# Two products trade places in the first group, and two heads trade buffers: a LoRA layer and paged attention on one core

## The chip, the core and the metric

The kernel runs on one core of a Trainium2 chip. A core has five engines that run side by side: TensorE (PE) for matrix products, VectorE (DVE), ScalarE (ACT), GpSimd (POOL) and SyncE (SP), which here only issues DMAs. ACT and POOL issue DMAs too. The metric is device time in microseconds for one execution, and the median over several runs is what counts.

## The reference

Two layers stand behind each other, each with a residual. For 8 sequences of 128 tokens with 512 features:

```python
x = x + einsum('bsi,boi->bso', x, weight[adapter_ids])      # one 512x512 adapter per sequence
# second layer, on the new x
q, k, v = x @ Wq.T, x @ Wk.T, x @ Wv.T                       # 32 query heads, 8 KV heads of 128
q, k = rope(rmsnorm(q, q_norm_w), pos), rope(rmsnorm(k, k_norm_w), pos)
k_all, v_all = concat(k_cache[block_table], k), concat(v_cache[block_table], v)   # 512 + 128 keys
probs = softmax(where(valid, q @ k_all.T * SCALE, -1e30))    # a cached key counts if below seqlen
x = x + (probs @ v_all).reshape(...) @ Wo.T
```

Everything is float32. Four query heads share one KV head.

## The kernel before

**Groups and steps.** The 8 KV heads are cut into 4 groups of 2, with 8 query heads each. A step is one group for one sequence, so there are 32 steps; step `i` has group `g = i // 8` and sequence `b = i % 8`. All sequences of a group come before the next group. Group 0 also does the first layer: its step `b` computes the first layer of sequence `b + 2` (`lora_y`, PE writes `y`, four matmuls in the source, eight on the chip, since a float32 product takes two passes).

**A step** has 8 heads, `h` = 0 to 7. Each head's scores (`sc`, L1037) go to PE; DVE adds the mask and takes the minimum (L1047), ACT takes the exponential (L1063), POOL divides by the sum (L1110), and DVE turns 32x32 blocks (`turn_p`, L886, to `tp`). Four heads of one KV head make a unit. When its fourth head is turned, SP sends four DMAs (`exchange`, L806) that finish the transposition from `tp` to `pT`. `pT` is 128 by 2560 floats, 1.3 MB.

**What PE does between the scores** is a list, `main`, whose pieces are dealt out over the 8 heads by a cost that is written into the code. For steps 1 to 5 its order is: the values of the first KV head of the step before (`values(i-1, 0)`: ten matmuls `o`, which read `pT`), the projections of the next step's keys and values and its first queries, `lora_y(b + 2)`, the values of the second KV head (`values(i-1, 1)`), the next step's second queries, and the output projection of the step before. In steps 6 and later (`early`) both values stand later. PE works through its list in this order; so does every other engine with its own.

**Buffers of turned probabilities.** The pool `pts` holds one `pT`. Up to step 4 both KV heads use it: the first head's `pT` of step `i`, which SP issues in head 5, must wait until `values(i-1, 1)` has read the last one; the second head's, issued in head 1 of the next step, waits for `values(i, 0)`. From step 5 on (`u.i >= B - 3`) there is a second buffer, the tile `raw` of the pool `lora`. It holds the adapter's rows until their last transposes (`turn_lora`, PE `lw`) in step 5. `move` picks the buffer.

**SP's order** in a step: in head 0 the second keys (`move_k(i, 1)`, `kT`), in head 1 the second queries (`qT`) and the last unit's `pT`, in head 4 the next step's first keys, in head 5 the first unit's `pT`, in head 6 the next step's first queries and new keys (`send_q`: DVE turns them to `tq`, L828, then four DMAs `qT<-tq`), and in group 0 x of a later sequence (`load_x(b + 3)`). SP waits in this order: a DMA behind a waiting one isn't issued. The new keys come with `qT`; ACT copies them into place (`copy_k`, L778) in head 7, and the next step's scores need that copy.

**Other transfers.** POOL gathers pages of the caches (`kc`, `vc`) and the adapter's rows (`gather_lora`, head 6); ACT loads, turns and stores weights for the next group.

Of the kernel before, what the change touches and what calls it, by code (L numbers as in the profile page):

```python
# [19 lines left out]
B = 8  # L20
# [32 lines left out]
def lora_then_paged_attention(  # L53
# [22 lines left out]
    def pool(name, bufs=1, **kw):  # L76
        return ctx.enter_context(tc.tile_pool(name=name, bufs=bufs, **kw))
# [5 lines left out]
    lora = pool("lora")  # L83
# [6 lines left out]
    pts = pool("pts")  # L90
# [45 lines left out]
    raw = {}  # L136


    first = {}
# [416 lines left out]
    def group(name, pieces, after, width=HID):  # L556

        y = [None]

        def piece(k, operands):  # L560
            if k == 0:
                if len(pending) > 1:
                    run(pending)
                y[0] = ps_mm.tile([P, HID], FP, tag="mm", name=name)[:, 0:width]
            lhsT, rhs = operands()
            nc.tensor.matmul(y[0], lhsT=lhsT, rhs=rhs, start=(k == 0), stop=(k == len(pieces) - 1))  # L566
            if k == len(pieces) - 1:
                after(y[0])

        return [(UNIT, lambda k=k, o=o: piece(k, o)) for k, o in enumerate(pieces)]  # L570
# [16 lines left out]
    def lora_y(b):  # L587
        def after(y):
            def add():
                a = acc[b].rearrange("s (p j) -> s j p", j=4)  # L590
                nc.vector.tensor_tensor(a, y.rearrange("s (j p) -> s j p", j=4), a, ALU.add)

            pending.append(add)

        return group(
            f"y_{b}",
            [
                lambda c=c: (x1T[b][:, c, :], wT["lora"][:, c, :, :].rearrange("k j p -> k (j p)"))
                for c in range(KC)
            ],  # L600
            after,
        )
# [107 lines left out]
    def project(i, what):  # L710
        g, b = steps[i]
        s = st[i]

        def after_kv(y):

            s.q[0] = work.tile([P, 4 + GK, D], FP, tag="q0", name=f"q_{i}_0")
            s.k = s.q[0][:, 4 : 4 + GK, :]
            s.vn = news.tile([P, GW], FP, tag="vn", name=f"vn_{i}")
            s.ss = [
                small.tile([P, 6], FP, tag=f"ss{n}", name=f"ss_{i}_{n}") for n in range(2)  # L720
            ]

            def rest():
                nc.scalar.copy(s.vn, y[:, GW : 2 * GW])
                rotate(i, y, s.k, s.ss[0][:, 4:6], 1, 0)

            pending.append(rest)

        def after_q(n):
            def after(y):  # L730
                if n:
                    s.q[n] = work.tile([P, 4, D], FP, tag=f"q{n}", name=f"q_{i}_{n}")

                def rest():
                    rotate(
                        i,
                        y,
                        s.q[n][:, 0:4, :],
                        s.ss[n][:, 0:4],
                        0,  # L740
                        n,
                        lambda: norm_scales(i, n, 6 if n == 0 else 4),
                    )

                pending.append(rest)

            return after

        after = after_kv if what == "kv" else after_q(int(what[1]))
        return group(  # L750
            f"pj_{i}_{what}",
            [lambda c=c: (x1T[b][:, c, :], weights_of(what, c)) for c in range(KC)],
            after,
        )
# [48 lines left out]
    def exchange(dst, src):  # L803

        for b in range(4):
            nc.sync.dma_start(  # L806
                out=dst[:, b, :].unsqueeze(1), in_=src[Q4 * b : Q4 * b + Q4, :, :]
            )
# [15 lines left out]
    def send_q(i, n):  # L824
        s = st[i]
        heads = 4 if n else 4 + GK
        tq = work.tile([P, 4, heads, Q4], FP, tag=f"tq{n}", name=f"tq_{i}_{n}")
        nc.vector.transpose(tq, s.q[n].rearrange("p h (a d) -> p a h d", a=4))  # L828

        def move():  # L830
            s.qT[n] = qT_tile(i, n)
            exchange(
                s.qT[n].rearrange("d b h q -> d b (h q)"), tq.rearrange("p a h q -> p a (h q)")
            )

        to_read.append((now[0], 0, move))
# [3 lines left out]
    def values(i, j, at_once=False):  # L840

        s = st[i]

        def operands(c):
            pT = s.pT[j].rearrange("p b r (c q) -> p c (b r) q", c=NC)
            v = s.vc[:, c, :] if c < LC else s.vn
            return v[:, j * D : (j + 1) * D], pT[:, c, :, :]

        def after(o):
            s.oT[j] = work.tile([P, REP, S], FP, tag=f"oT{j}", name=f"oT_{i}_{j}")  # L850

            def copy():
                nc.scalar.copy(s.oT[j].rearrange("p h s -> p (h s)"), o)  # L853

            if at_once:
                copy()
            else:
                pending.append(copy)

        return group(f"o_{i}_{j}", [lambda c=c: operands(c) for c in range(NC)], after)  # L860

    def output(i, half=None):
        g, b = steps[i]
        s = st[i]
        cols = slice(0, 16) if half is None else slice(8 * half, 8 * half + 8)
        return group(
            f"out_{i}",
            [
                lambda h=h: (s.oT[h // 4][:, h % 4, :], weights_of(f"o{h // 4}", h % 4)[:, cols, :])
                for h in range(GQ)  # L870
            ],
            add_to_acc(b, g == G - 1, half),
            HID if half is None else HID // 2,
        )
# [26 lines left out]

    def move(u):

        pl, tag = (lora, "raw") if u.j and u.i >= B - 3 else (pts, "pT")
        pT = pl.tile([P, 4, REP, QK], FP, tag=tag, name=f"pT_{u.i}_{u.j}")
        exchange(pT.rearrange("p b r k -> p b (r k)"), u.tp.rearrange("p a r k -> p a (r k)"))
        st[u.i].pT[u.j] = pT
# [79 lines left out]
    for i, (g, b) in enumerate(steps):  # L987
        s = st[i]
        main = []
# [17 lines left out]
            main += values(i - 1, 0)  # L1007
        if i == last:
            main += output(i - 2)
        if g == 0 and b + 2 < B and i:  # L1010
            main += lora_y(b + 2)
        if i and not early:
            main += values(i - 1, 1)
        if i < last:
            main += project(i + 1, "q1")
        if early and i < last:
# [9 lines left out]
        for h in range(8):  # L1026
# [39 lines left out]
            if prev is not None:  # L1066
                u, pr = prev
                if u.i < last or u.j == 0:
                    turn_p(u, pr)
                if pr == REP - 1:  # L1070
                    to_read.append((8 * i + h, 1, lambda u=u: move(u)))
# [116 lines left out]
```

## Time and profile before

| | us |
|---|---|
| median of three runs (1225.03 to 1226.6) | 1226.48 |
| the profiled execution | 1226.99 |
| its span, first to last instruction | 1225.2 |
| PE busy | 1183.1 |
| DVE, ACT, POOL busy | 745.4, 534.4, 674.0 |
| PE busy with scores (L1037) | 324.7 |
| steps 2 to 5, length of each | 49.5, 48.9, 47.4, 47.3 |
| a step of group 1 (400.00 to 437.70) | 37.7 |

PE's mean granted clock is 0.987 of full speed. A row of a timeline gives the start, the length, the engine, the line of the kernel and the operation with its output and inputs; "SPq" is SP issuing a DMA, whose length is the time to issue, not to land. In brackets stands how long the engine was idle before and what ended the wait. A row of windows gives the stretch, its length, each engine's busy time and instructions, the granted clock, the DMA engines' busy share and what they moved. Names such as `pT` cover every tile of that name. The records of DMA packets in the trace have a queue, a start, a length and a size, and the sizes tell the transfers apart (`pT` 2560 bytes, `qT` with keys 768, `kT` 512, x 2048, the adapter's rows 8192).

### The profile page before, as it was taken

The page shows a single profiled execution, that of the slowest core. Times are in us where ns is not written, and L with a number is a line of the kernel's source. Part 1 is how long each engine was busy: PE and PEld are TensorE (multiplying, and loading weights), DVE is VectorE, ACT ScalarE, POOL GpSimd, SP SyncE. Part 2 cuts the span into 40 slices and gives each one's busy share as a digit, 9 for nine tenths or more (in the row PEclk, how much of TensorE's full clock was granted, in tenths as well). Part 3 has the DMA queues.
Part 4 walks back from the last instruction along what each step waited for, and adds up shares of the span by engine and source line. Part 5 has one row for each costly group of instructions (what it writes and reads, how often), then busy time and mean ns, then how long its engine had stood idle before and what let it go on. Part 6 is the DMA issues. An engine that isn't in the chain of part 4 may idle for free.

```text
span 1225.2 us, 13384 instructions
## 1 busy us (share of the span) xinstructions
PE 1183.1 (97%) x3354; PEld 577.5 (47%) x3354; DVE 745.4 (61%) x1675; ACT 534.4 (44%) x1648; POOL 674.0 (55%) x780
## 2 busy tenths in 40 slices
PE   7898979889899999999999999999999999999998
PEld 5553544444444444444444444444444444444445
DVE  5565646355556776666666776766666656656651
ACT  4563433434344444444444444444444444444442
POOL 5465445254465666555565666555566666555541
PEclk9999989889999999999999999999999999999999
DMA  7376466565597797767797787766797776655642
GB/s 283 104 192 172 122 177 169 156 169 134 142 236 178 205 250 192 176 173 201 171 241 183 203 254 187 177 182 189 174 238 181 184 201 148 150 138 149 150 116 60
DMA packets 173952, 217.59 MB, mean 178 GB/s; under 512 B 19508, under 2 KB 112436, under 8 KB 172980
## 3 DMA queue, kind: packets, MB, share of 16 engines
q1 hardware_dynamic: 111072, 128.76, 45.5%
q10 hardware_dynamic: 49524, 48.12, 12.4%
q0 software_dynamic: 13280, 39.86, 10.1%
q8 instruction: 28, 0.46, 0.2%
q14 instruction: 48, 0.39, 0.1%
HBM read 80.74 MB, written 17.83 MB: 80 GB/s over the span
## 4 chain that ended last, share of the span: by engine, by line
PE 92%; DMA 4%; ACT 1%; SPq 1%; DVE 1%; issue 1%; POOL 0%; ACTq 0%; DVEq 0%; POOLq 0%
PE sc L1037 23%; PE o L566 23%; PE pj_q L566 18%; PE out L566 15%; PE pj_kv L566 9%; DMA qT<-tq 3%; PE y L566 2%; PE lw L481 1%; DMA kT<-tk 1%; PE x L481 1%; SPq L806 1%; DVE p L1047 0%; PE wt_q L499 0%; PE wt_kv L499 0%; PE qt L793 0%
## 5 line engine op out<-in xcount | busy, mean ns | idle before, releaser
L1047 DVE CUSTOM_DVE_ANT_0 p<-sc,mask 128x640 f32<-128x640 f32 x256 | 210.9, 824 | 383.9 <-PE sc L1037 383.5
L1063 ACT ACTIVATE p<-p,mn 128x640 f32<-128x640 f32 x256 | 211.9, 828 | 331.6 <-DVE mn L1047 321.2
L1037 PE MATMUL sc<-kT,qT 128*128 128x512 f32 (+1 forms) x1024 | 324.7, 440 | 26.8 <-ACT kT L778 25.8
L1110 POOL TENSOR_SCALAR p<-p,rc 128x640 f32<-128x640 f32 x252 | 201.6, 800 | 268.6 <-DVE rc L1103 264.4
L1037 PEld LDWEIGHTS sc<-kT,qT 128*128 128x128 f32 x1024 | 194.2, 193 | 262.2 <-issue 226.9
L566 PE MATMUL o<-pT,vc 128*128 128x512 f32 x512 | 239.1, 597 | 0.0
L566 PE MATMUL pj_q<-w_q,x1T 128*128 128x512 f32 x512 | 236.8, 593 | 0.7 <-ACT w_q L500 0.7
L566 PE MATMUL out<-w_o,oT 128*128 128x512 f32 (+1 forms) x528 | 235.0, 580 | 0.9 <-ACT oT L853 0.7
L886 DVE STREAM_TRANSPOSE tp<-p 128x640 f32<-128x640 f32 x252 | 210.8, 836 | 4.1 <-POOL p L1110 3.9
L685 POOL TENSOR_TENSOR q<-q,sw 128x512 f32<-128x512 f32 (+1 forms) x89 | 96.8, 1087 | 98.8 <-DVE sw L668 98.6
L617 POOL DMA_INDIRECT kc<-in_L_cond_k_cache_dram,key_ix x128 | 130.7, 1021 | 32.8 <-issue 32.5
L617 POOL DMA_INDIRECT vc<-in_L_cond_v_cache_dram,val_ix x128 | 127.3, 995 | 31.1 <-issue 29.9
L566 PEld LDWEIGHTS out<-w_o,oT 128*128 128x128 f32 x528 | 95.7, 190 | 93.5 <-issue 85.4
L566 PEld LDWEIGHTS pj_q<-w_q,x1T 128*128 128x128 f32 x512 | 92.4, 190 | 92.7 <-issue 90.1
L566 PEld LDWEIGHTS o<-pT,vc 128*128 128x128 f32 x512 | 93.1, 193 | 89.8 <-issue 87.9
L698 ACT ACTIVATE q<-q,rs 128x128 f32<-128x128 f32 x256 | 81.8, 390 | 106.0 <-POOL q L685 93.9
L566 PE MATMUL pj_kv<-w_kv,x1T 128*128 128x512 f32 x256 | 116.6, 593 | 0.7 <-ACT x1T L483 0.7
L651 ACT ACTIVATE sq<-pj_q 128x128 f32<-128x128 f32 x256 | 70.7, 276 | 64.7 <-PE pj_q L566 39.7
L693 POOL TENSOR_TENSOR rs<-ss,mhalf 128x6 f32<-128x6 f32 x64 | 77.0, 1203 | 5.3
L566 PEld LDWEIGHTS pj_kv<-w_kv,x1T 128*128 128x128 f32 x256 | 46.0, 190 | 45.6 <-issue 44.7
L566 PE MATMUL o<-pT,vn 128*128 128x512 f32 x128 | 65.4, 593 | 0.0
L1103 DVE RECIPROCAL rc<-sm 128x1 f32<-128x1 f32 x256 | 33.4, 130 | 46.0 <-ACT p L1063 46.0
(123 smaller groups left out, 834.3 us busy)
## 6 DMA issues: line engine op xcount, KB each, us to landing
pT<-tp SPq DMA_DIRECT2D x252, 320.0 KB
kT<-tk SPq DMA_DIRECT2D x248, 64.0 KB
qT<-tq SPq DMA_DIRECT2D x116, 96.0 KB
qT<-tq SPq DMA_DIRECT2D x120, 64.0 KB
st_q<-in_L_cond_Wq_dram ACTq DMA_DIRECT2D x24, 256.0 KB
xw_q<-tw_q ACTq DMA_DIRECT2D x24, 256.0 KB
st_o<-in_L_cond_Wo_dram ACTq DMA_DIRECT2D x24, 256.0 KB
xw_o<-tw_o ACTq DMA_DIRECT2D x24, 256.0 KB
```

Of the source, the lines that this page charges most:

```text
L566: nc.tensor.matmul(y[0], lhsT=lhsT, rhs=rhs, start=(k == 0), stop=(k == len(pieces) - 1))
L617: nc.gpsimd.indirect_dma_start(out=dst[:, c, :], out_offset=None, in_=src, in_offset=bass.IndirectOffsetOnAxis(ap=rows[:, g, at : at + 1], ...
L651: nc.scalar.activation(sq, t[:, h, :], AF.Square, scale=float(D) ** -0.5, accum_out=ss[:, h : h + 1])
L685: add.tensor_tensor(dst, cw, sw[:, 0:heads, :], ALU.add)
L693: nc.gpsimd.tensor_tensor(rs[:, 0:width], ss[:, 0:width], mhalf[:, 0:width], ALU.pow)
L698: nc.scalar.activation(q, q, AF.Identity, scale=rs[:, h : h + 1])
L886: nc.vector.transpose(u.tp[:, :, r, :], u.p.pop(r).rearrange("q (a k) -> q a k", a=4))
L1037: nc.tensor.matmul(sc[:, lo:hi], lhsT=s.qT[j][:, r, 0:4, :].rearrange("d h q -> d (h q)"), rhs=s.kT[j].rearrange("d a c i -> d (a c i)")[: ...
L1047: nc.vector.tensor_tensor_reduce(out=p, in0=sc[:, 0:LA], in1=mask.rearrange("p a c i -> p (a c i)"), scale=1.0, scalar=3.0e38, op0=ALU.add ...
L1063: nc.scalar.activation(p, p, AF.Exp, bias=unit.mn[:, one], scale=-1.0, accum_out=unit.sm[:, one])
L1103: nc.vector.reciprocal(unit.rc[:, one], unit.sm[:, one])
L1110: nc.gpsimd.tensor_scalar(q, p, unit.rc[:, one], 1.0, ALU.mult, ALU.mult)
```

## The change

In steps 1 to 4 `values(i-1, 1)` comes ahead of `lora_y(b + 2)`. In step 5 (`b + 3 == B`) the order stays. From step 5 on the buffer `raw` takes the first KV head's `pT` and the buffer of `pts` the second's, where it was the other way round. Steps 0 and 6 to 31 keep their order.

```diff
     def move(u):
 
-        pl, tag = (lora, "raw") if u.j and u.i >= B - 3 else (pts, "pT")
+        pl, tag = (lora, "raw") if u.j == 0 and u.i >= B - 3 else (pts, "pT")
         pT = pl.tile([P, 4, REP, QK], FP, tag=tag, name=f"pT_{u.i}_{u.j}")
...
         if i == last:
             main += output(i - 2)
-        if g == 0 and b + 2 < B and i:
-            main += lora_y(b + 2)
+        first = lora_y(b + 2) if g == 0 and b + 2 < B and i else []
+        if b + 3 == B:
+            main += first
         if i and not early:
             main += values(i - 1, 1)
+        if b + 3 < B:
+            main += first
         if i < last:
             main += project(i + 1, "q1")
```

## The prediction

> **What bounds the kernel now.** I read the page first: PE is busy 1183.1 of 1225.2 us, so only its 42.1 us of idling can be won, plus what a lowered clock costs. Then PE's waits: one line holds 25.8 us of the 42.1.
>
> ```profile
> PE sc L1037 <- ACT kT L778: 25.8, 5, 6.6
> ```
>
> Five times PE waits for ACT's copy of the new keys (`copy_k`, L778). PE's timeline puts them ahead of the first scores of steps 2 to 6: 5.19, 6.38, 6.57, 3.94 and 3.68 us. Here is step 2 (from 121.48 us) up to the second of them; columns are start, length, engine, line, operation.
>
> ```profile
> 141.67 1.88 PE L566 MATMUL y<-wT,x1T 128*128 128x512 f32 x4
> 144.91 1.88 PE L566 MATMUL y<-wT,x1T 128*128 128x512 f32 x4
> 146.62 2.74 PE L566 MATMUL o<-pT,vc 128*128 128x512 f32 x6
> 149.20 1.24 PE L1037 MATMUL sc<-kT,qT 128*128 128x512 f32 x4
> 150.28 1.02 PE L566 MATMUL o<-pT,vc 128*128 128x512 f32 x2
> 151.14 1.02 PE L566 MATMUL o<-pT,vn 128*128 128x512 f32 x2
> 161.03 3.60 PE L566 MATMUL out<-w_o,oT 128*128 128x512 f32 x8
> 171.00 2.50 PE L1037 MATMUL sc<-kT,qT 128*128 128x512 f32 x4 [6.38 <-ACT kT L778]
> ```
>
> The first layer's product `y` runs, then the second KV head's values `o`, done at 152.16; PE runs dry at 164.63. SP's issues in the same stretch:
>
> ```profile
> 131.96 5.50 SPq L806 DMA_DIRECT2D pT<-tp  x4
> 140.18 2.48 SPq L806 DMA_DIRECT2D kT<-tk  x4
> 152.19 5.00 SPq L806 DMA_DIRECT2D pT<-tp  x4
> 157.30 5.73 SPq L806 DMA_DIRECT2D qT<-tq  x4
> 163.07 0.61 SPq L104 DMA_DIRECT2D acc<-in_x_dram  x1
> 163.78 5.86 SPq L806 DMA_DIRECT2D kT<-tk  x4
> ```
>
> The turned probabilities of step 2's first heads (`pT`, 152.19) go out 0.03 us after `o` has ended, though their source `tp` was ready at 148.21 (DVE, L886, 147.38 and 0.83 long): the one buffer of `pts` still held the last step's second heads. The next step's queries (`qT`) stand behind `pT` in SP's order; their packets end at 169.72, and ACT's copy, which needs the keys in them, starts at 170.54. (ACT's row names `kT<-tk` there; but in all five cases the copy follows `qT`'s last packet by 0.6 to 0.8 us.) Last, the steps and their sums (length, busy PE, PEld, DVE, ACT, POOL, granted clock, DMA share, GB/s):
>
> ```profile
> 121.48:171.00 49.52, 43.15 (x124) 21.68 (x125) 25.93 (x53) 18.52 (x56) 21.43 (x24) 0.91 0.62 168
> 171.00:219.86 48.86, 42.30 (x124) 21.11 (x125) 26.66 (x54) 18.47 (x56) 21.61 (x24) 0.95 0.59 158
> 219.86:267.26 47.40, 43.45 (x125) 21.79 (x125) 24.85 (x53) 18.47 (x56) 21.44 (x24) 0.93 0.59 158
> 267.26:314.58 47.32, 43.64 (x125) 21.90 (x125) 24.73 (x52) 18.57 (x56) 20.67 (x23) 0.93 0.57 143
> 314.58:353.40 38.82, 38.15 (x101) 18.44 (x102) 22.08 (x52) 17.74 (x56) 22.54 (x26) 0.96 0.68 183
> 400.00:437.70 37.70, 37.70 (x103) 17.84 (x102) 26.85 (x61) 16.73 (x54) 21.58 (x25) 1.00 0.81 210
> ```
>
> After each wait PE runs at half clock for a while (2 us windows show 0.50): four scores take 2.29 us to the next operation instead of 1.08. A step of this kind needs 40.7 us of PE at full clock; what the first four rows hold above that is the clock: 2.45 + 1.6 + 2.75 + 2.95 us, and some 1.5 us in the fifth. So the boundaries cost 25.8 + 0.7 (a wait of 0.67 us for x1T behind the last) + 11.2 = **37.7 us**.
>
> **The change part by part.**
>
> *Values ahead of `y` in steps 1 to 4.* No instruction is added or dropped: ten `o` matmuls and eight `y` matmuls (0.43 us apart, `y` 3.44 us in all) trade places; neither issues a DMA, and PE's total is unchanged: zero. `o` now begins where `y` did and all of it fits ahead of the sixth head's scores (1.08 us), so it ends 4.5 us earlier: 99.3, 147.6, 196.3 and 246.3 us on the clock of the traced run, instead of 103.8, 152.2, 200.8 and 250.9.
>
> *What that releases.* `pT` then waits for `tp` instead (ready at 99.0, 148.2, 196.9, 246.9). So SP issues it at 99.3, 148.2, 196.9, 246.9: 4.5, 4.0, 4.0, 4.0 us sooner. Its 5 us of issuing end at about 104.3 to 251.9, just when `tq`, the source of `qT`, is ready (104.64, 153.79, 201.75, 251.98), so `qT` is issued 4.2, 3.5, 4.0 and 4.2 us sooner.
>
> *The buffers trade places from step 5.* No work is added. In step 5 the first heads' `pT` no longer waits for the values at 298.43; it needs the last transposes of the adapter's rows (`lw`, 289.66 and 0.60 long) and `tp` (294.49): 4.0 us sooner, `qT` 4.5 us sooner. From step 6 each head has one buffer as before: zero.
>
> *What that does at PE.* From `pT`'s issue to the scores took 17.6, 18.8, 19.0, 16.4 and 16.1 us; PE runs dry 17.0, 16.4, 16.4, 16.4, 16.4 us after the new issues. Worst end: `qT` keeps its time from issue to landing; then waits of 1.0, 2.9, 2.6, 0 and 0 us remain, 6.5 us. Best end: none. I take none, because the sources of the delay thin out: between 144 and 146 us the DMA engines move nothing and in 148 to 154 a third of their time, while in 154 to 170 they are 0.9 busy with `pT`, `qT`, the gathers for steps ahead and x at once. `pT` took 9.7 us of packets there, and 7.7 us where it was alone (133.16 to 140.83). The gathers are POOL's and keep their places relative to PE, so `pT` and `qT` go ahead of them.
>
> *What is late next.* (1) Just behind `qT` on SP comes x of the step after, used 1.5 us into the new step. Before, it ended 0.7 to 3.3 us after `qT`. The adapter's gather (1 MB; 164.34 to 169.68 us, POOL) is first turned some 4.5 us into the step. With the boundary closed these come 0 to 1.2 us late in four steps. They share one wait; I take 0.5 each, the middle: 2 us. (2) `o` now starts 10.7, 9.7, 9.7 and 9.7 us after its own `pT` was issued (131.96 against 141.67). That `pT`'s packets ended 9.8, 8.9, 8.8 and 8.4 us after issue, and a reader starts 0.6 to 0.8 us later: it just fits. In steps 6 and 7 the same transfer took 10.0 and 9.6 us (322.65 to 332.64, 341.06 to 350.67), so 0 to 1 us late: 0.5 each, 2 us. While PE waits there, `y`, the next projections and scores queue behind it, but all that they feed moves with them.
> (3) `y`'s addition on DVE (1.1 us, L591) moves out of the fifth head into the seventh, where DVE idles 1.7 to 3.4 us: zero; uncovered, 1.1 us a step. The copy of `o` on ACT (0.59 us) moves ahead by a head into 2.9 us of idle time: zero. The first layer's result is read only in the next step.
>
> *Does a short wait cost the clock?* The waits of 3.68 to 6.57 us all did; none shorter is in these steps, so the residual may cost from nothing up to 1.5 to 3 us each. In 2 us windows the clock falls 2.7 to 5.3 us after PE stops, so for half a microsecond I take nothing. The Trainium skill (TensorE: Matmul & The Clock Gate, Why this matters for your kernels) says the rate halves after idle gaps above about 3 us; the trace agrees with its 3.68 us. By that rule the worst end above stays free of it too.
>
> **Sum.** 37.7 - 2 - 2 = 33.7 us off the profiled execution's 1226.99 us (its span is 1225.2): 1193.3. The median of the three runs, 1226.48, is 0.5 lower: **1193 us**. Nothing below 1226.5 - 37.7 = 1188.8 can come of this.
>
> **Rivals.**
> *Fixed delays.* The queries' time from issue to landing stays and 6.5 us of boundary waits remain, with the 2 us at the values, and the two longer ones (2.9, 2.6) may still lower the clock for 1.6 to 2.95 us each: 37.7 - 8.5 - (0 to 5) = 24 to 29, so 1197 to 1202. For it: `qT`'s issue alone took 4.5 to 6.1 us behind `pT` against 2.48 when free. Against: the idle DMA time at 144 to 154.
> *DMA becomes the bound.* Shorter steps push about 8.3 MB (168 GB/s by 49.5 us) through 41 us: 203 GB/s. The values' `pT` then takes 11.4 us, the longest seen (299.67 to 311.11), and `o` waits 2.5 us in four steps, with 1.2 us for x or the adapter: 15 us, plus up to 8 us of clock: 1204 to 1212. Against: later steps move 210 GB/s at share 0.81 with PE never idle (last row above). The Trainium skill (DMA: Bandwidth & Descriptors, Issuing engines are not separate DMA queues) has all queues interleave on the same engines, which speaks for this one; the trace shows that too, as `qT` took 8.9 us of packets beside the adapter's gather.
> *Slower.* One mechanism could turn the sign: `o` of the second head stands ahead of everything in PE's order and waits for its own `pT`, which is still in flight, where `y` used to cover 3.44 us. It decides from a lateness of about 6.5 us a step (four times 6.5 and the clock's 2.5 to 3 make up 37.7). A `pT` would need 16 us; the longest row is 11.4. At 17 us it would give 1229.
> *It does not do what it says.* `pT` stays tied to something that ends with 152.2. I see only `tp`, 4 us earlier: 1226.5.
>
> **Chances.** Forecast 0.60 (1189 to 1196), fixed delays 0.20, DMA bound 0.11, slower 0.05, no change 0.04. The range from 1187 to 1206 leaves out most of the third and both last. What a measurement here can tell from no change is about 0.2%, 2.5 us: faster 0.91, same 0.04, slower 0.05.
>
> **What would show it.** Right: no line of PE waiting for L778 above some 5 us in all, steps 2 to 5 at 41 to 42 us, clock 1.00 at their starts, SP's second `pT` issue 4 us nearer to the sixth head's scores. Wrong: a new PE line at L566 `o` waiting for DMA `pT`, or at L481 for `lraw` or x, or `pT` issued late for another reason.

## The result

The changed kernel takes 1191.97 us (median of 4 runs, 1190.25 to 1193.39) against 1226.54 for the kernel before (4 runs, 1225.03 to 1237.19): a ratio of 0.9691, 95% interval 0.9661 to 0.9722. The prediction was 1193. The profiled execution took 1193.18 us (span 1191.3), 33.8 less than the one before.

### The profile after

PE is busy 1172.7 of 1191.3 us. PE's waits, the line that led before being gone:

```profile
engine line waited for: us in total, times, longest us
PE spread L391 <- DVE row_f L395: 6.1, 1, 6.1
PE lw L481 <- DMA lraw<-in_L_cond_weight_dram,lora_ix: 2.4, 1, 2.4
```

No line of PE names the keys' copy (L778) any more. The prologue's 6.1 us were there before. New is one wait of 2.4 us for the adapter's rows. The steps 1 to 6 in windows, columns as before (length, then busy PE, PEld, DVE, ACT, POOL, granted clock, DMA share, GB/s):

```profile
74.14:116.13 41.99, 41.99 (x138) 21.70 (x139) 26.66 (x55) 20.39 (x59) 24.07 (x27) 1.00 0.70 186
116.13:160.87 44.74, 42.34 (x126) 21.10 (x125) 25.57 (x53) 18.33 (x55) 21.55 (x25) 0.96 0.65 178
160.87:201.33 40.46, 40.46 (x125) 20.18 (x124) 25.29 (x55) 18.42 (x55) 21.53 (x25) 1.00 0.74 194
201.33:241.80 40.47, 40.47 (x126) 20.18 (x124) 24.67 (x55) 18.30 (x55) 21.56 (x25) 1.00 0.74 192
241.80:282.26 40.46, 40.46 (x125) 20.18 (x124) 25.61 (x55) 18.46 (x55) 21.68 (x25) 1.00 0.69 184
282.26:318.04 35.78, 35.10 (x97) 16.70 (x96) 21.77 (x52) 17.06 (x54) 21.77 (x25) 1.00 0.71 185
```

In steps 3 to 5 PE is never idle and never slowed: 40.46 us is what such a step costs. Steps 1 to 5 got shorter by 5.4, 4.8, 8.4, 6.9 and 6.9 us, and step 6 by 1.6 (it ran from 314.58 to 351.92 before, 37.3 us). That is 33.9 us, the whole difference of the spans; nothing was given back later.

Two stretches shown in the prediction were not what they were called. `314.58:353.40` reached 1.5 us into step 7, and `400.00:437.70` is no step: later steps take 34.4 us (351.92 to 386.32 before, 352.45 to 386.85 after). What was argued from them, the rate of the transfers and PE without idling, stands.

SP's issues in step 2, which starts at 116.13 us now:

```profile
128.36 5.54 SPq L806 DMA_DIRECT2D pT<-tp  x4
136.59 2.48 SPq L806 DMA_DIRECT2D kT<-tk  x4
144.69 5.26 SPq L806 DMA_DIRECT2D pT<-tp  x4
150.05 4.21 SPq L806 DMA_DIRECT2D qT<-tq  x4
154.31 0.90 SPq L104 DMA_DIRECT2D acc<-in_x_dram  x1
```

The fifth head's scores start at 140.23 here and at 143.82 before. The first heads' `pT` (second `pT` row) follows them by 4.5 us now and by 8.4 before: 3.9 us sooner. `qT` follows by 9.8 instead of 13.5. ACT's copy, which the new step waits for, then comes in time; its row now names `qT` itself:

```profile
159.17 0.43 ACT L778 COPY kT<-qT 128x128 f32<-128x128 f32 x1 [3.46 <-DMA qT<-tq]
```

It ends at 159.60, 1.3 us ahead of the scores at 160.87. Step 2 on PE, where the one new wait stands, and the values that now come ahead of `y`:

```profile
116.13 1.24 PE L1040 MATMUL sc<-kT,qT 128*128 128x512 f32 x4
117.21 1.04 PE L481 MATMUL x<-ident,acc 128*128 128x128 f32 x8
118.08 2.74 PE L566 MATMUL o<-pT,vc 128*128 128x512 f32 x6
123.22 1.03 PE L481 MATMUL lw<-ident,lraw 128*128 128x128 f32 x4 [2.40 <-DMA lraw<-in_L_cond_weight_dram,lora_ix]
124.05 2.34 PE L1040 MATMUL sc<-kT,qT 128*128 128x512 f32 x4
...
138.07 1.88 PE L566 MATMUL o<-pT,vc 128*128 128x512 f32 x4
...
141.31 1.88 PE L566 MATMUL o<-pT,vc 128*128 128x512 f32 x4
143.03 1.02 PE L566 MATMUL o<-pT,vn 128*128 128x512 f32 x2
143.89 1.88 PE L566 MATMUL y<-wT,x1T 128*128 128x512 f32 x4
```

The adapter's gather had its packets from 116.57 to 122.59. The scores behind the wait take 2.13 us to the next operation instead of 1.08: 42.34 busy against 40.46 says that the lowered clock cost 1.9 us on top of 2.4.

### The profile page after: what moved, and what is told of

The parts are those of the page before. It is cut to its first block, busy times and chain, and to the rows that moved or that the text cites. A ratio compares the mean times of both kernels' runs of the same rounds, so it can differ in the third digit from the quotient of the medians.

```text
span 1191.3 us, 13375 instructions
## 1 busy us (share of the span) xinstructions
PE 1172.7 (98%) x3354; PEld 572.0 (48%) x3354; DVE 743.9 (62%) x1675; ACT 534.0 (45%) x1648; POOL 674.1 (57%) x780
## 4 chain that ended last, share of the span: by engine, by line
PE 96%; POOL 1%; DMA 1%; ACT 1%; DVE 1%; issue 1%; DVEq 0%; ACTq 0%; POOLq 0%
PE sc L1040 23%; PE o L566 23%; PE pj_q L566 18%; PE out L566 18%; PE pj_kv L566 9%; PE y L566 2%; PE lw L481 1%; DMA lraw<-in_L_cond_weight_dram,lora_ix 1%; PE x L481 1%; PE wt_q L499 0%; PE wt_kv L499 0%; PE qt L793 0%; PE wt_o L499 0%; POOL kc L617 0%; POOL vc L617 0%
## 5 line engine op out<-in xcount | busy, mean ns | idle before, releaser
L1040 PE MATMUL sc<-kT,qT 128*128 128x512 f32 (+1 forms) x1024 | 319.5, 434 | 1.1 <-ACT kT L773 0.8
L651 ACT ACTIVATION_READ_ACCUMULATOR sq<-pj_q 128x1 f32 x256 | 49.7, 194 | 0.0
```

What stands on the lines that cost most here:

```text
L651: nc.scalar.activation(sq, t[:, h, :], AF.Square, scale=float(D) ** -0.5, accum_out=ss[:, h : h + 1])
L1040: nc.tensor.matmul(sc[:, lo:hi], lhsT=s.qT[j][:, r, 0:4, :].rearrange("d h q -> d (h q)"), rhs=s.kT[j].rearrange("d a c i -> d (a c i)")[: ...
```

## The experiments

Each kernel below was timed beside the kernel before on the same chip, whose median there was 1227.97 to 1229.28 us; the ratios are against that.

### One part at a time

**The order alone.** The exchange of the buffers is undone:

```diff
-        pl, tag = (lora, "raw") if u.j == 0 and u.i >= B - 3 else (pts, "pT")
+        pl, tag = (lora, "raw") if u.j and u.i >= B - 3 else (pts, "pT")
```

> The order of the products changed, the buffers left as they were. My theory (the queries wait on SP behind pT, and pT waits for its one buffer): the waits for the keys' copy go at steps 2 to 5, and the fifth, ahead of step 6, stays with its 3.7 us and about 1.5 us of lowered clock, so some 5 us above the changed kernel: 1197 us. Rival (the order alone shortens the whole stretch, and the buffers' exchange is cosmetic): 1192 us, no such wait left.

Measured 1197.8 us (1193.12 to 1201.92, ratio 0.973, interval 0.970 to 0.976). Its profile has one wait for the copy left, the fifth, 3.3 us long:

```profile
PE lw L481 <- DMA lraw<-in_L_cond_weight_dram,lora_ix: 3.6, 3, 2.1
PE sc L1040 <- ACT kT L778: 3.3, 1, 3.3
```

**The buffers alone.** The kernel before with that line alone:

```diff
-        pl, tag = (lora, "raw") if u.j and u.i >= B - 3 else (pts, "pT")
+        pl, tag = (lora, "raw") if u.j == 0 and u.i >= B - 3 else (pts, "pT")
```

> The buffers exchanged, the order of before. My theory: only the wait ahead of step 6 goes, 3.7 us and about 1.5 us of lowered clock: 1221 us, with four waits of 4 to 7 us left ahead of steps 2 to 5. Rival (the second buffer is what frees the first heads in all steps): clearly under 1215 us.

Measured 1220.97 us (1217.5 to 1227.91, ratio 0.9947, interval 0.9921 to 0.9973). Four waits are left, of 3.31, 6.58, 6.41 and 3.34 us, and the one ahead of step 6 is gone:

```profile
PE sc L1037 <- ACT kT L778: 19.6, 4, 6.6
```

So the two parts do not overlap: the order closes four boundaries, the exchange the fifth.

**The order in step 5 too, instead of the exchange.** The changed kernel with the values ahead in all of steps 1 to 5, and the buffers as before:

```diff
-        if b + 3 == B:
-            main += first
         if i and not early:
             main += values(i - 1, 1)
-        if b + 3 < B:
-            main += first
+        main += first
```

> The values ahead of the first layer's product in step 5 too, and the buffers left as they were. My theory says the exchange of the buffers and the order do the same thing at step 6, letting pT out 4 us sooner: no wait for the keys' copy ahead of steps 2 to 6, 1192 us within 2. Rival (in step 5 the values then wait for their own pT, or the exchange does more than free a buffer): 1195 us or more, with a wait at o or the 3.7 us still there.

Measured 1191.47 us (1190.19 to 1192.15, ratio 0.9689, interval 0.9665 to 0.9713), with no wait for L778. At step 5 either way of letting `pT` out does.

### Is it the buffer that holds the first heads back?

**A second buffer, no reordering.** The kernel before with two buffers in `pts`. One rotary table of 4 KB stands in for the four to make room, so queries and keys are turned by the wrong angles; no instruction is dropped.

```diff
-    pts = pool("pts")
+    pts = pool("pts", 2)
...
-    CW = const.tile([P, 2, B, D], FP, name="CW")
-    SW = const.tile([P, 2, B, D], FP, name="SW")
+    CW = const.tile([P, 1, B, D], FP, name="CW")
+    SW = CW
```

> The kernel before, in its order, with a second buffer of the same kind for pT (pts has two). To make room, one rotary table stands in for the four, so queries and keys are turned by the wrong angles; every instruction stays. My theory (it is the buffer's release that holds pT back): pT goes out when its source is ready, 4 us sooner in steps 1 to 5, all waits for the keys' copy go or shrink under 1 us, and the time is that of the changed kernel, 1188 to 1194 us, without any reordering. Rival (it matters that the values, not the first layer's product, run there, or where the transfers fall between the others): 1205 us or more.

Measured 1192.77 us (1191.44 to 1193.65, ratio 0.971, interval 0.9676 to 0.9743). With `y` still ahead of the values, the copy is never waited for:

```profile
PE lw L481 <- DMA lraw<-in_L_cond_weight_dram,lora_ix: 2.7, 3, 1.4
```

In step 2 SP now issues the first heads' `pT` as soon as `tp` is ready (141.96), while the last step's `o` still runs; before, it went out only after `o` had ended:

```profile
142.00 5.32 SPq L806 DMA_DIRECT2D pT<-tp  x4
144.89 1.02 PE L566 MATMUL o<-pT,vn 128*128 128x512 f32 x2
```

That shows the cause most directly. What counts is when the buffer comes free for SP; beyond that these runs show no gain from the order on PE (ratio 0.971 here, 0.9691 and 0.9701 for the changed kernel). The second buffer also does one thing that the order does not: the second heads' `pT` goes out sooner, 6.6 us after step 2's first scores instead of 12.2 in the changed kernel. The run with the order alone lacks that, and its first four waits went all the same.

**The queries ahead of the late transfer.** The kernel before, with the first heads' `pT` issued one head later, so that `qT` passes it on SP:

```diff
-                    to_read.append((8 * i + h, 1, lambda u=u: move(u)))
+                    to_read.append((8 * i + h + (0 < u.i < B - 2 and u.j == 0), 1, lambda u=u: move(u)))
...
-            to_read[:] = [r for r in to_read if r[0] == 8 * i + h]
+            to_read[:] = [r for r in to_read if r[0] >= 8 * i + h]
```

> The kernel before, with SP issuing the first heads' pT of steps 1 to 5 one head later, behind the next queries instead of ahead of them; nothing else moves. My theory (the queries are late because they stand behind a pT that waits): the waits for the keys' copy go; pT, issued at about 156.3 instead of 152.2 in step 2, ends some 14 us after the sixth head's scores, just when its reader starts, so up to 1 or 2 us may be waited at o in five steps: 1190 to 1202 us. Rival (the DMA engines are full there, and the queries come when the bytes are through, in whatever order they are issued): waits of 3 us and more for the keys' copy remain, 1205 to 1225 us.

Measured 1221.56 us (1216.29 to 1228.93, ratio 0.9949, interval 0.9922 to 0.9976). The time lies in the rival's range, but not by the rival's means. The wait for the keys' copy is gone in all five places, so the queries were late for standing behind `pT`. But x, the next in the line, took it over:

```profile
PE x L481 <- DMA acc<-in_x_dram: 19.6, 4, 7.4
```

and the fifth boundary, which has no x behind it, closed without a wait. In step 2 `qT` was through at 153.29, `pT` only at 166.29 and x at 166.94, on the heels of `pT`. I had priced `pT` and its reader and forgotten what is queued behind `pT` on SP.

### What the new order risks

**The second heads' transfer later.** Two tries. The first puts it one head later in SP's program:

```diff
-                    to_read.append((8 * i + h, 1, lambda u=u: move(u)))
+                    to_read.append((8 * i + h + (u.i < 4 and u.j == 1), 1, lambda u=u: move(u)))
```

(with the same second edit as above).

> The changed kernel, with SP issuing the second heads' pT one head later in steps 1 to 4 (in head 2 instead of head 1), about 4.9 us. This prices the wait that the new order risks. My theory (that transfer just fits): o of the second heads waits for its pT, about 4 us in each of four steps, with some 1.5 to 3 us of lowered clock after each: 16 to 28 us above the changed kernel, 1208 to 1220 us. Rival (there is more room than the packets' ends suggest): under 1200 us, with waits below 2 us.

Measured 1193.65 us (1190.64 to 1198.41, ratio 0.971, interval 0.9675 to 0.9745), and it says nothing on the question: in step 1 SP issued that `pT` 8.50 us after the step's first scores in both kernels. SP has no other work between heads 1 and 2 and waits for the first heads' `o` in either place. The second try puts it behind the next step's first keys, which wait for the fourth head's scores:

```diff
-                if pr == REP - 1:
+                if pr == REP - 1 and u.j and u.i < 4:
+                    held.append(u)
+                elif pr == REP - 1:
...
-            if h == 4 and i < last:
+            if h == (3 if held else 4) and i < last and moved != i:
                 move_k(i + 1, 0)
+                if held:
+                    move(held.pop())
+                    moved = i
```

> The changed kernel, with the second heads' pT of steps 1 to 4 put on SP behind the next step's first keys, whose issue waits for the fourth head's scores: some 11 us later (12 in the first), so it is issued about 1 us after its reader o could start. (One head later, tried before, moved nothing: SP has nothing else to do in between and waits for o of the first heads either way.) This prices the wait that the new order risks. My theory, by the prediction's arithmetic: o of the second heads waits about 10 us in each of four steps, with 2 to 3 us of lowered clock behind each: 45 to 55 us above the changed kernel, 1235 to 1247 us, slower than before. Rival (the boundaries take part of it back, since the transfers for the next step get time while PE waits): below 1226 us.

Measured 1245.33 us (1244.35 to 1246.5, ratio 1.0133, interval 1.0091 to 1.0175), slower than the kernel before.

```profile
PE o L566 <- DMA pT<-tp: 41.3, 4, 10.7
```

Steps 1 to 4 take 53.3, 54.5, 54.1 and 54.0 us, 52.5 more than the 42.0 and three times 40.46 without waits. Of that 41.3 are these waits, 1.9 two short ones for the adapter, and the rest, 9.3, is the clock that each of them lowers. Nothing is recovered at the boundaries. So the slower rival was a real mechanism, and it is the 9.7 us between issue and use that keep it away.

### The wait that is left

**The adapter's gather in head 5**, ahead of the keys' pages:

```diff
+                if g == 0 and i and h == 5 and b + 3 < B:
+                    gather_lora(b + 3)
                 if i + 1 < last and h in ((3, 5) if i else (4, 5)):
...
                 load_x(b + 3)
-                gather_lora(b + 3)
+                if not i:
+                    gather_lora(b + 3)
```

> The changed kernel, with POOL gathering the adapter's rows in head 5 instead of head 6 in steps 1 to 4, ahead of the keys' pages instead of behind the values'. My theory: the one wait that is left ahead of a turned adapter (2.4 us and about 1.9 us of lowered clock in step 2 of the profiled execution) goes in every execution, and nothing else waits: 1188 to 1189 us, all runs alike. Rival (the megabyte then collides with pT or the queries, which share the DMA engines): a wait for the keys' copy comes back, 1192 us or more.

Measured 1203.42 us (1202.76 to 1213.3, ratio 0.9821, interval 0.9785 to 0.9857). The rival was right: the wait for the adapter is gone and the copy's is back, as a megabyte now runs beside the queries (their packets took 8.8 us in step 1 against 4.3 in the changed kernel).

```profile
PE sc L1040 <- ACT kT L778: 9.6, 4, 3.3
```

**The gather in head 6, ahead of the values' pages** instead of behind them (the old call goes as above):

```diff
+                if g == 0 and i and h == 6 and b + 3 < B:
+                    gather_lora(b + 3)
                 for c in {6: (0, 1), 7: (2, 3)}.get(h, ()) if i else (range(LC) if h == 7 else ()):
```

> The changed kernel, with POOL gathering the adapter's rows ahead of the values' pages within head 6, some 2.6 us sooner, but behind the keys' pages and the queries' issue. My theory (in head 5 the megabyte collided with the queries; here it starts when they are nearly through): the wait ahead of the turned adapter goes and no wait for the keys' copy comes: 1188 to 1190 us. Rival (any megabyte ahead of the queries' landing delays them): waits of 1 us and more for the keys' copy, 1192 us or more.

**PE turning the adapter one head later**, no transfer moved:

```diff
-                at(i, c if i else c + 2, False, lambda b=b, c=c: turn_lora(b + 2, c))
+                late = int(0 < b < B - 3)
+                at(i, c + late if i else c + 2, False, lambda b=b, c=c: turn_lora(b + 2, c))
```

> The changed kernel, with PE turning the adapter's rows one head later in steps 1 to 4 (heads 1 to 4 instead of 0 to 3), which the first layer's later product now allows. No transfer moves. My theory (what is left are waits of up to 2.4 us for the adapter's rows, about 5 us before their use could be): no wait for them in any execution, 1188 to 1189 us, all runs within 1 us. Rival (the rows' buffer comes free a head later and something else takes the wait's place): 1191 us or more.

**The changed kernel again**, beside them:

> The changed kernel again, on the chip of the other runs of this call: 1190 to 1194 us, with a wait of 0 to 3 us for the adapter's rows in step 2, 3 or 4 that comes and goes between executions.

Measured: gather ahead of the values 1191.97 us (1189.4 to 1194.21, ratio 0.9694), turned later 1193.68 (1192.75 to 1198.24, ratio 0.9716), changed kernel again 1192.04 (1190.95 to 1198.24, ratio 0.9701). By the total none is better, and the first two missed the times that were expected of them. In its one profiled execution the first did at PE what was expected: no wait for the adapter or the copy, steps 1 to 5 at 42.0 and four times 40.5, and from step 1's first scores to the end 1113.3 us against 1117.2 and 1117.5 for the two executions of the changed kernel. What hides it is the start: step 1's first scores fall at 77.01 us in it and at 74.14 and 78.95 in those two, so the prologue varies by 5 us, more than the 4 us to be won. With one execution against two, the gain is a hint and not shown. Turning later took the wait for the rows away too, but steps 1 to 4 grew to 42.7, 42.1, 41.5 and 41.2: `y` now waits 0.5 us in three of them for the turned rows, and in one `o` 0.6 us for its `pT`. These waits are what its rival named; the total, 1191 us or more as the rival said, does not decide, as the changed kernel beside it took that long too.

The changed kernel's own waits for the adapter were 2.4 us once in one profiled execution and 1.1, 1.1 and 1.3 us in the other: they come and go with the transfers.

## Why the prediction was right

**What the boundaries cost.** 37.7 us were forecast as 25.8 of waiting, 0.7 behind the last and 11.2 of clock. With 40.46 for a step instead of my 40.7, the clock was 12.3 (2.69 + 1.84 + 2.99 + 3.18, and 1.57 in step 6). The 0.7 (x1T), which I had counted among what would go, stayed. So 25.75 + 12.27 = 38.0 us could be won.

**The release of the buffer.** Held, and is shown by three runs: the order alone, the exchange alone and the second buffer without either. `pT` was issued 3.9 us sooner in step 2 (forecast 4.0) and 4.5 in step 1 (99.34 against 103.85, forecast 4.5).

**Nothing left of the queries' wait.** I took the best end against a worst one of 6.5 us because the DMA engines had idle time earlier. That was right: `qT`'s packets took 4.3, 6.0 and 6.3 us in steps 1 to 3 against 8.4, 8.9 and 9.2, and the copies ended 3.7, 1.3, 1.5 and 1.7 us ahead of need. The run with the adapter's gather in head 5 shows how little is spare: there all four waits were back.

**What is late next.** Here the terms were mis-sized, and they cancelled. (1) I had 0.5 us at four boundaries, 2 us, for x or the adapter. It was 2.4 us once, and 1.9 of clock, which I had put at nothing for a wait of half a microsecond. x was never late. (2) I had 0.5 us at four values, 2 us; there was no wait. `pT`'s packets ended at 92.59, 137.16, 177.81 and 218.12, and `o` started 0.7 to 0.9 us later each time, without idling: "it just fits" was exact. So 38.0 less 4.3 is 33.7, and the measured difference 33.8. That 33.7 was also the forecast is luck: four errors cancelled (0.7 too much and 1.1 too little in what could be won, 2.3 too little for the adapter, 2 too much for `o`). The wait at L481 for `lraw` that the prediction named as a sign of being wrong did come, but in the profiled execution in one step and not in four.

**The rule on the clock.** The prediction leaned on the Trainium skill (TensorE: Matmul & The Clock Gate, Why this matters for your kernels), whose limit is idle gaps above about 3 us. The runs do not agree: waits of 1.94, 2.08 and 2.40 us lowered it, and one of 3.18 us did not.

**The rivals.** Fixed delays: no wait was left. DMA as the bound: not at these rates (194 GB/s at share 0.74 in step 3), though the gather in head 5 shows the queries losing to other bytes. Slower: priced at 1229 us for a transfer of 17 us; with some 20 us from the usual issue to use it gave 1245. No change: `pT` was tied to nothing else and went out when forecast.

## What to carry to other kernels

An engine that issues DMAs in a written order passes a wait on to all that stands behind it: here a buffer's late release made the queries late, which do not use that buffer, and moving the queries ahead only passed the bill to x. Look for what the last reader of a single buffer is queued behind, and either read earlier or add a buffer; both gave the same time. Before reordering readers, measure from issue to last packet of what they read: here 9 us had to fit into 9.7.

## What the runs showed of the hardware

Waits of 1.94 us and more could lower PE's clock, and the fall could come after PE was at work again. In the second heads' first try, PE idled from 166.73 to 168.67:

```profile
166.00:168.00 2.00, 0.73 (x2) 0.00 (x0) 1.14 (x3) 0.53 (x2) 1.52 (x2) 1.00 0.51 145
168.00:170.00 2.00, 1.33 (x6) 0.96 (x7) 0.00 (x0) 0.58 (x1) 0.04 (x1) 0.85 0.55 153
170.00:172.00 2.00, 2.00 (x5) 0.97 (x5) 0.75 (x3) 0.00 (x0) 0.00 (x0) 0.50 0.03 8
```

A mean of 0.85, if the clock falls once from 1.00 to 0.50, puts the fall at 169.4, 2.7 us after the idling began and 0.7 after it had ended. It cost 1.9 us, as much as the wait. From step 1 on, waits up to 1.5 us cost no clock in the profiled executions. Two longer ones cost none either, 2.69 us (the gather in head 5, ahead of step 5) and 3.18 us (the queries ahead, in step 2), so the length alone does not decide.

The trace's own record of the clock points to what else does. In each of the 13 profiled executions the recorded clock changed only at points a whole number of 3.41 us apart, and its low stretches, but for one cut off by the end of the record, lasted 3.41, 6.83, 10.24 or 13.65 us. That fits a wait of some 2 to 3 us costing one such stretch or none, by where it falls between two points; no run moved a wait to test it.

The start of the program varied too: from the first instruction to step 1's first scores 74.1 to 79.0 us. In the two executions that needed 77.0 us the record has a clock of 0.50 from 13.4 to 20.2 us. In the two that needed 78.9 to 79.0 it begins only at 22.6 us (9.9 to 11.9 in the others), and the first `y` products took 6.0 us instead of 3.67, so a low clock is the likely cause there as well, though the record does not show it.
